# Reordered ScalarE copies and queue writes around the weighted sums, and a shorter last whitening chain

## The chip, the cores and the metric

The kernel runs on one core of one Trainium2 chip. The metric is device time in microseconds (us) of one execution. The profile is that of one further execution, taken by the hardware profiler.

## What is computed

Two layers follow each other. The first is a local attention with learned weights: for every pixel, 49 weights come from two convolutions and a softmax, and they weight the 49 dilated neighbours of that pixel.

```python
# x: (4, 256, 64, 64) f32; w1: (128, 256, 7, 7); w2: (49, 128, 1, 1)
k = conv(x, w1, rhs_dilation=(2, 2), padding 6) + b1
k = conv(k, w2) + b2
attn = softmax(k, axis=1)
xp = pad(x, 6)
shifts = stack([xp[:, :, 2*u:2*u+64, 2*v:2*v+64] for u in range(7) for v in range(7)], axis=1)
x = einsum('bkchw,bkhw->bchw', shifts, attn)
```

The second layer whitens the 256 channels in 4 groups of 64, over all 16384 pixels of the 4 images (m = 16384):

```python
x = x.transpose(1, 0, 2, 3).reshape(4, 64, -1)
xc = x - mean(x)
Sigma = 1e-5 * I + xc @ xc.T / m
rTr = 1 / trace(Sigma);  SN = Sigma * rTr;  P = I
for _ in range(5):
    P = 1.5 * P - 0.5 * (P @ P @ P) @ SN
out = (P * sqrt(rTr)) @ xc * weight + bias
```

## The kernel before

Dilation 2 splits an image into even and odd rows and columns, so the kernel works on 16 parts (`n`, four for each image `b`), each a quarter of an image. The two convolutions are merged into one 7x7 convolution with 49 outputs, and that one is run in a transformed domain: six transformed rows for each image (`ROWS`), each in three banks of transformed columns (`BANKS`, `i` = 0, 1, 2), plus one row that is computed directly (`direct_inf`).

- **Convolution step** (`conv_step`, L828). `conv_bank` (L577) issues the matmuls of a bank (L603) into one of two PSUM buffers `cv`, and ScalarE copies the result to `pv` (L614, L619). `prepare` (L819) makes weights and inputs for the same bank of the next row on VectorE: `row_eval` (L488; for row 0 it has two copies on ScalarE, L510, one for each of the two row parities), `col_eval` (which leaves a copy of one input to ScalarE, L545 or L551), `weights` (L403; for image 1 they are also scaled on ScalarE, L481, and stored for reuse by a DMA on SP, L482). The copies and scalings are put into a list `points` and issued after the eviction of the next bank (L625). VectorE then interpolates (`col_interp`, `row_interp`, L345 to L352).
- **Softmax** (`softmax`, L1037). TensorE transposes the logits (L1009), ScalarE takes exponentials (L1049), VectorE normalises and shuffles (L997).
- **Weighted sums**, part by part. `move_terms` (L1095) lays the weights out in `zt` with eleven copies (L1127, on ScalarE for images 0 to 2), and eight DMAs write them to memory (`sd`, L1146, on GpSimd's queue POOL; for part 12 half of them on SP). `load_band` (L1182) reads them back as bands through SP (L1196, L1208). `first_half` and `second_half` (L1453, L1492) transpose blocks of x (L1252), which ScalarE copies to `xb` and to the edge tiles `xbz` (L1283, L1274); multiply them with the bands (L1316); and store the sums in place of x (L1338).
- **Moments**. `turn_y` (L1382) transposes the stored sums (L1388), ScalarE copies them to `yt` (L1398), and `moments` adds their products to `sig` in PSUM (L1407). In each image one part is closed at once by `finish` (L1444); the others are closed inside the next `first_half`. When the two parts of a tile of x are closed, `move` (L1426) writes the tile to memory (`spill`, 2 MB, POOL) and reads a later image into its place (`slot<-ahead`, 2 MB, L159, POOL).
- **Order of the work.** The parts' steps are planned into gaps between the convolution steps (`plan`, `gap`, L1516 to L1589), eight gaps to an image. Each engine's order is fixed when the program is built: a scheduler takes what is ready, first what stands in `tc.high_priority()`; TensorE keeps program order.
- **End.** After the last convolution the remaining parts run without convolution steps between them (L1616 to L1664). Then two whitening chains (`whiten`, L1706), one for each half of the channels, go through short steps on TensorE, ScalarE and VectorE. The first is filled with the remaining sums (`units`); the second runs between the matmuls of the output (L1701), whose results ScalarE and VectorE scale (L1830, L1836), and SP writes out (L1842, 33 DMAs from six buffers).

Of the kernel before, what the change touches and what calls it, by code (L numbers as in the profile page):

```python
# [32 lines left out]
def kernel(  # L33
# [31 lines left out]
    P = 128  # L65
# [508 lines left out]

    later, points = [], []

    def conv_bank(b, br, i, w):  # L577
# [34 lines left out]
        with tc.high_priority():  # L612
# [5 lines left out]
            if INF in pts:  # L618
# [5 lines left out]
                )  # L624
        for waiting in (points, later) if i == 1 else (points,):  # L625
            while waiting:
                with tc.high_priority() if waiting is points else nullcontext():
                    copied = waiting.pop()()
                for one in copied if isinstance(copied, list) else [copied]:
                    tc.add_manual_dep(  # L630
                        one.ins,
                        last.ins.name,
                        mybir.DependencyInfo(
                            mybir.DependencyClass.NoSync, mybir.DependencyReason.DATA
                        ),
                        reason="later",
                    )

# [189 lines left out]
    def conv_step(k, i):  # L828
        w = {bc: nxt.pop(bc) for bc in BANKS[i]}
        b, br = rows[k]  # L830
        conv_bank(b, br, i, w)
        end = b > 0 and br == ROWS[-1]
        if end:

            with in_order():
                if i == len(BANKS) - 2:
                    col_interp(b, br, 0)
                elif i == len(BANKS) - 1:
                    col_interp(b, br, 1)
                    row_interp(b, 1)  # L840
        last = i == len(BANKS) - 1 and br == ROWS[-2]
        if k + 1 < len(rows):
            with tc.high_priority() if last else nullcontext():
                prepare(k + 1, i, points.append)
# [250 lines left out]
    def move_terms(n, after=None):  # L1095
# [46 lines left out]
        for g in range(CR):  # L1142
            for h in range(2):
                p0 = g * SW + h * TC
                queue = nc.sync if h and n == 4 * (B - 1) else nc.gpsimd
                dma = queue.dma_start(  # L1146
                    bass.AP(
                        tensor=D.tensor,
                        offset=D.offset + h * HS + g * RS,
                        ap=[[LS, TC], [CR * RS, NCH], [1, KS * WS]],  # L1150
                    ),
                    zt[p0 : p0 + TC, R : R + NCH * KS].rearrange(
                        "p (m e) w -> p m (e w)", e=KS
                    ),
                )
                if queue is nc.gpsimd:
                    written[:] = [dma]
# [285 lines left out]

    def finish():  # L1444

        n = open_n.pop()
        for t8 in (2, 3):
            turn_y(n, t8)
        moments(n, 1)
        if n % 2:  # L1450
            move(n // 2)

    def first_half(n):  # L1453
        last = open_n.pop() if open_n else None

        def turn(t8):
            if last is not None:
                turn_y(last, t8)
# [12 lines left out]
        turn(3)  # L1471
        weighted_sum(n, 0, 3)
        weighted_sum(n, 0, 4)
        move_terms(n + 1, store_y(n, 0))
        half_done.add(n)
        load_band(n + 1, 0)
        make_blocks(n, 3, y_dve.get((n, 0))) if (n, (3, 0)) not in blocks else None
        if last is not None:
            moments(last, 1)
            if last % 2:  # L1480
                move(last // 2)

    def bands(n, after=None):
# [7 lines left out]

    def second_half(n, mid=None):  # L1492
        turned = turn_y(n, 0)
        if n % 4 == 3:
            bands(n + 1, turned)
        weighted_sum(n, 1, 0)
        weighted_sum(n, 1, 1)
        turn_y(n, 1)
        weighted_sum(n, 1, 2)
        weighted_sum(n, 1, 3)  # L1500
        weighted_sum(n, 1, 4)
        if mid is not None:
            mid()
        last = store_y(n, 1)
        if n + 1 < 4 * B:
            make_blocks(n + 1, 0, y_dve.get((n, 1)))
        moments(n, 0)
        open_n.append(n)
        done.add(n)
        bands(n + 1, last)  # L1510
# [25 lines left out]
    for b in range(B):  # L1536
# [5 lines left out]
        if b + 2 < B:  # L1542
            for j in range(8):
                plan(b + 1, 2 + j, hs[j])
                if j == 3:

                    plan(b + 1, 2 + j, finish)
        else:
            for j in range(8):
                if b == B - 1 or 3 + j >= NPC:  # L1550
                    rest.append(hs[j])
                else:
                    plan(b + 1, 3 + j, hs[j])
    for b in range(B - 1):
        for j in range(2) if b else ():
            plan(b + 1, b * j, lambda b=b, j=j: soft(b, j))

    slots[4] = store[4]
    pieces = read_x(halves(store[4]), 4, nc.sync)
# [7 lines left out]
    for b in range(1, B):  # L1567
# [13 lines left out]
        j, at, whole = 0, 0, sum(c for c, _ in steps)  # L1581
        for cost, f in steps:
            f()
            while rest_of:
                rest_of.pop()()
            at += cost
            if at * NPC >= (j + 1) * whole:
                gap(b, j)
                j += 1  # L1589
    apool.release()  # L1590
    rpool = ctx.enter_context(tc.tile_pool(name="rp", bufs=1, reuse_waits="tile"))
# [32 lines left out]
    rest[2]()  # L1624
    finish()
    soft_start(1, False)
    move_terms(n + 2)
    for t8 in range(4):
        if (n, (t8, 0)) not in blocks:
            make_blocks(n, t8)  # L1630
    rest[3]()
    rest[4]()
# [21 lines left out]
    with tc.issue_after(stored.ins):  # L1654
# [17 lines left out]
        lambda: turn_part(0, 1, 0),  # L1672
        lambda: turn_part(0, 1, 1),
        lambda: turn_part(1, 1, 0, 0),
        lambda: turn_part(1, 1, 1, 0),
        lambda: moments_part(0, 1, (0, 1)),
# [16 lines left out]
    nc.vector.tensor_tensor(own, ident[:, :GW], ident[:, GW:], ALU.add)  # L1693
    nc.vector.tensor_scalar(eps, own, EPS, None, ALU.mult)
    nc.vector.tensor_scalar(i15, own, 1.5, None, ALU.mult)
    wm, wmx, sc, beta = {}, {}, {}, {}

    def parts_mm(t, lhs, rhs, crossed=False):
        for i, o in ((G0, G1 if crossed else G0), (G1, G0 if crossed else G1)):
# [4 lines left out]
            )  # L1704

    def whiten(cc):  # L1706

# [4 lines left out]
        G = sig[:, cc]  # L1712
        nmu = work.tile([P, 1], F32, tag="nmu", name=f"nmu{cc}")
        nc.scalar.mul(nmu, G[:, GW : GW + 1], -1.0 / NPIX)
        D = small(f"D{cc}")
        nc.scalar.activation(D, own, AF.Copy, scale=nmu)
        dt_ = small(f"dt{cc}")
        nc.vector.tensor_tensor(dt_, G[:, :GW], own, ALU.mult)
        dg = work.tile([P, 1], F32, tag="dg", name=f"dg{cc}")
        nc.vector.tensor_reduce(dg, dt_, AX.X, ALU.add)  # L1720
        mu = work.tile([P, 1], F32, tag="mu", name=f"mu{cc}")
        nc.vector.tensor_scalar(mu, G[:, GW : GW + 1], 1.0 / NPIX, None, ALU.mult)
        nc.vector.tensor_scalar(dg, dg, 1.0 / NPIX, EPS, ALU.mult, ALU.add)
        traced = nc.vector.scalar_tensor_tensor(dg, mu, nmu, dg, ALU.mult, ALU.add)
        fill()
# [8 lines left out]
        with tc.issue_after(traced.ins):  # L1734
            nc.vector.scalar_tensor_tensor(S, G[:, :GW], 1.0 / NPIX, eps, ALU.mult, ALU.add)
        nc.vector.scalar_tensor_tensor(S, t[:, :GW], mu, S, ALU.mult, ALU.add)
        rtr = work.tile([P, 1], F32, tag="rtr", name=f"rtr{cc}")
# [9 lines left out]
        for it in range(1, T_ITERS):  # L1747
# [10 lines left out]
            fill()  # L1758
            yield

# [5 lines left out]
        q = work.tile([P, 1], F32, tag="q", name=f"q{cc}")  # L1766
        nc.scalar.activation(q, rtr, AF.Sqrt)
# [4 lines left out]
        ab = work.tile([P, 2], F32, tag="ab", name=f"ab{cc}")  # L1772
        scale = ab[:, 0:1]
# [30 lines left out]
    for cc in range(NCC):  # L1804
        for b in (3, 2, 1, 0):
# [3 lines left out]
            for k, (r0, nr) in enumerate(rows):  # L1809
# [4 lines left out]
                for pr in range(2):  # L1814
# [62 lines left out]
```

## Time and profile before

| What | Value |
|---|---|
| Median of 3 runs | 682.57 us (680.88 to 682.58) |
| Profiled execution, its own time | 680.68 us |
| its span | 678.7 us |
| TensorE clock granted, mean | 0.996 |
| VectorE busy | 566.3 us (83%) |
| ScalarE busy | 332.7 us (49%) |
| Output DMAs, first issue to the end of the span | 632.5 us to 678.7 us |
| Spill of a 2 MB tile, issue to landing | 9.8 us (the one at 253.3 us) |
| Reload of a 2 MB tile, issue to landing | 9.7 us (the one at 263.6 us) |

The profiled execution took 2.0 us more than its span; that is what lies before and after the traced work. In a timeline, each line is a run of like instructions with its start, its length and, in brackets, how long the engine was idle before it and what ended that. In a table of windows, each line is a stretch with the busy time and instruction count of every engine, the clock, and how busy the 16 DMA engines were. Ends of matmuls are modelled, so a short wait can be hidden inside a busy stretch.

### The profile page before, as it was taken

The page shows a single profiled execution, that of the slowest core. Times are in us where ns is not written, and L with a number is a line of the kernel's source. Part 1 is how long each engine was busy: PE and PEld are TensorE (multiplying, and loading weights), DVE is VectorE, ACT ScalarE, POOL GpSimd, SP SyncE. Part 2 cuts the span into 40 slices and gives each one's busy share as a digit, 9 for nine tenths or more (in the row PEclk, how much of TensorE's full clock was granted, in tenths as well). Part 3 has the DMA queues.
Part 4 walks back from the last instruction along what each step waited for, and adds up shares of the span by engine and source line. Part 5 has one row for each costly group of instructions (what it writes and reads, how often), then busy time and mean ns, then how long its engine had stood idle before and what let it go on. Part 6 is the DMA issues. An engine that isn't in the chain of part 4 may idle for free.

```text
span 678.7 us, 19071 instructions
## 1 busy us (share of the span) xinstructions
PE 648.2 (96%) x7800; PEld 527.6 (78%) x7800; DVE 566.3 (83%) x1240; ACT 332.7 (49%) x862; POOL 117.2 (17%) x177
## 2 busy tenths in 40 slices
PE   6999999999999999999899999999999999999993
PEld 1439573357899988889899998999899999998430
DVE  3699999999389889999999589989998987633673
ACT  1424331023565555566755554464854566634663
POOL 0000550662213020001122020002130203400000
PEclk9999999999999999999999999999999999999998
DMA  8961899993599979313587485027374325649698
GB/s 318 248 162 67 138 262 361 217 185 50 116 208 224 228 160 370 120 60 84 166 269 245 139 279 189 2 67 190 94 199 111 71 63 123 166 98 384 237 404 354
DMA packets 110607, 126.09 MB, mean 186 GB/s; under 512 B 69255, under 2 KB 91896, under 8 KB 109368
## 3 DMA queue, kind: packets, MB, share of 16 engines
q1 hardware_dynamic: 93528, 69.03, 35.3%
q0 software_dynamic: 10944, 37.57, 22.1%
q10 hardware_dynamic: 6048, 18.27, 8.8%
q8 instruction: 61, 1.00, 0.6%
q14 instruction: 26, 0.21, 0.1%
HBM read 78.78 MB, written 52.36 MB: 193 GB/s over the span
## 4 chain that ended last, share of the span: by engine, by line
PE 67%; DVE 19%; ACT 6%; DMA 4%; issue 2%; POOL 0%; ACTq 0%; DVEq 0%; SPq 0%; POOLq 0%
PE cv L603 24%; PE y L1316 10%; PE cv L770 8%; PE acc L770 8%; PE sig L1407 4%; PE tp L1388 3%; DMA out_dram<-out 3%; PE tp L1252 2%; DVE pv L352 2%; DVE zz L352 2%; PE cv L251 2%; DVE xh L352 2%; DVE ct L352 2%; DVE zz L348 1%; DVE zz L345 1%
## 5 line engine op out<-in xcount | busy, mean ns | idle before, releaser
L603 PE MATMUL cv<-xh,wr 128*49 128x128 f32 x4160 | 232.6, 273 | 0.2
L603 PEld LDWEIGHTS cv<-xh,wr 128*49 128x49 f32 x4160 | 226.1, 124 | 3.3 <-issue 1.0
L1146 POOL DMA_DIRECT2D sd<-zt x124 | 65.2, 532 | 334.6 <-ACT zt L1127 269.6
L1316 PE MATMUL y<-band,xb 128*128 128x209 f32 x448 | 93.9, 342 | 4.7 <-ACT xb L1283 2.7
L1316 PEld LDWEIGHTS y<-band,xb 128*128 128x128 f32 x448 | 75.7, 190 | 6.0 <-ACT xb L1283 3.3
L614 ACT COPY pv<-cv 113x486 f32<-113x486 f32 (+2 forms) x60 | 26.0, 433 | 90.6 <-PE cv L603 90.3
L352 DVE SCALAR_TENSOR_TENSOR pv<-pv 113x162 f32<-113x162 f32 x176 | 53.1, 322 | 2.2 <-ACT pv L614 1.4
L1127 ACT COPY zt<-d 32x112 f32<-32x112 f32 (+2 forms) x132 | 38.5, 292 | 14.9 <-DVE d L997 9.3
L1398 ACT COPY yt<-tp 128x512 f32<-128x512 f32 x60 | 34.9, 593 | 21.1 <-PE tp L1388 20.5
L1388 PE MATMUL tp<-ident,slot 128*128 128x128 f32 x240 | 41.5, 296 | 1.0 <-ACT slot L1338 1.0
L1049 ACT ACTIVATE d<-tp,mx 128x49 f32<-128x49 f32 x96 | 27.5, 322 | 28.0 <-DVE mx L1046 28.0
L1252 PE MATMUL tp<-ident,slot 128*128 128x128 f32 x256 | 40.5, 282 | 0.0
L1407 PE MATMUL sig<-yt 128*64 128x65 f32 x1024 | 38.1, 225 | 2.3 <-ACT yt L1398 2.3
L1388 PEld LDWEIGHTS tp<-ident,slot 128*128 128x128 f32 x240 | 34.9, 205 | 6.1 <-issue 3.8
L1407 PEld LDWEIGHTS sig<-yt 128*64 128x64 f32 x1024 | 32.9, 137 | 8.2 <-ACT yt L1398 3.0
L1252 PEld LDWEIGHTS tp<-ident,slot 128*128 128x128 f32 x256 | 38.1, 204 | 0.2 <-issue 0.2
L1283 ACT COPY xb<-tp 128x512 f32<-128x512 f32 x52 | 30.5, 586 | 9.7 <-PE tp L1252 6.6
L352 DVE SCALAR_TENSOR_TENSOR xh<-ct 128x512 f32<-128x512 f32 x40 | 26.5, 692 | 10.2 <-PE cv L603 9.9
L770 PE MATMUL acc<-slot,tap 128*49 128x256 f32 (+7 forms) x224 | 34.7, 468 | 0.0
L770 PEld LDWEIGHTS acc<-slot,tap 128*49 128x49 f32 x224 | 16.0, 123 | 18.0 <-issue 15.5
L147 POOL DMA_DIRECT2D slot<-in_x_dram x12 | 20.4, 1700 | 53.8 <-DVE xh L352 38.2
L348 DVE TENSOR_TENSOR pv<-pv 113x162 f32<-113x162 f32 (+1 forms) x77 | 27.5, 366 | 0.3
(258 smaller groups left out, 1141.2 us busy)
## 6 DMA issues: line engine op xcount, KB each, us to landing
out_dram<-out SPq DMA_DIRECT2D x31, 512.0 KB, 5.9
band<-sd SPq DMA_DIRECT2D x64, 242.0 KB, 3.7
sd<-zt POOLq DMA_DIRECT2D x124, 77.0 KB, 3.3
wr<-gd ACTq DMA_DIRECT2D x14, 588.0 KB, 5.0
wr<-gd ACTq DMA_DIRECT2D x14, 490.0 KB, 4.8
slot<-in_x_dram POOLq DMA_DIRECT2D x12, 512.0 KB, 10.5
ahead<-in_x_dram POOLq DMA_DIRECT2D x12, 512.0 KB, 7.5
spill<-slot POOLq DMA_DIRECT2D x3, 2048.0 KB, 10.5
```

Source lines behind the costliest of these rows:

```text
L348: return in_turn(TT(o, a, b, ALU.subtract))
L352: return in_turn(STT(o, a, f, b, ALU.mult, ALU.add))
L603: nc.tensor.matmul(o, wv[:, sc, sr, cc], xv[bc][:, h * NCC + cc], start=(j == 0), stop=(j == len(terms) - 1), skip_group_check=True,)
L770: nc.tensor.matmul(ps[h * HB : h * HB + KT, :, o0:o1], w[v][:, cc], rhs, start=(j == 0 and k == 0), stop=(j == len(order) - 1), skip_group ...
L1127: ins = nc.scalar.copy(o, i)
L1146: dma = queue.dma_start(bass.AP(tensor=D.tensor, offset=D.offset + h * HS + g * RS, ap=[[LS, TC], [CR * RS, NCH], [1, KS * WS]],), zt[p0 : ...
L1252: nc.tensor.transpose(t[:, h * C + cc * P : h * C + (cc + 1) * P], tile_of(xt, cc, t8, h, pc), turned_by(n),)
L1283: (nc.vector.tensor_copy if n > 4 * B - 3 else nc.scalar.copy)(xb.rearrange("p a c -> p (a c)"), t[:, : 2 * C])
L1316: nc.tensor.matmul(y_ps[n, half, cc][:, q0 : q0 + nq, c0:c1], xb[:, cc * P : (cc + 1) * P], rhs, start=(k == 0), stop=(k == len(PIECES[hal ...
L1388: nc.tensor.transpose(t[:, h * C + cc * P : h * C + (cc + 1) * P], tile_of(yt, cc, t8, h, pc), turned_by(n),)
L1398: return nc.scalar.copy(yb.rearrange("p h a g c -> p (h a g) c")[:, :, :GW], t[:, : 2 * C].rearrange("p (e c) -> p e c", c=GW),)
L1407: nc.tensor.matmul(sig[g * GW : (g + 1) * GW, cc], yb[:, g, :GW], yb[:, g], start=(count[0] == 0), stop=end, skip_group_check=True,)
```

## The change

It touches the order around the weighted sums, the POOL and SP queues, and the end. No matmul, tile size or buffer count is changed.

1. **Held copies.** When the gap after a step holds one half of a part's sums (`half_gaps`), the copies and scalings in `points` are no longer issued behind the eviction ahead of that gap. They go to `held`, and `give_out` issues them after a `turn_y` or a store inside the half. For the first bank of row 0 of an image, `prepare` itself is called after such a gap (`after_gap`).
2. **Closing a part.** `finish` is called inside `second_half` (`close=True`), ahead of the `move_terms` of the next part, no longer as a step of its own after it. So ScalarE copies `yt` before `zt`, and the spill and the reload move up in POOL's queue: the spill now stands ahead of the eight `sd` writes of parts 3 and 7, and the reload behind the first of them and ahead of the other seven.
3. **Part 4** writes half of its eight `sd` pieces through SP, as part 12 did.
4. **First block.** The block transpose and `xb` copy of part 0 are planned one gap earlier.
5. **After the convolutions.** One part's last moments are put after the sums of the following first half (`ends`), so the logits' transposes come earlier.
6. **Whitening.** The negated mean is dropped; the mean is scaled so that the division by the pixel count falls out, which drops an operation on ScalarE and one on VectorE ahead of the trace. Two one-column operations are added (on `qi`, and `down`), and the last two operations for `beta` become one. Two `turn_part` copies go from ScalarE to VectorE.
7. **Fillers.** The last two fillers stand behind output tiles 2 and 3 instead of 1 and 2, and the second chain skips one output tile and drops its last stop.

In the built program the instruction counts of TensorE stay at 4215. On ScalarE 808 instructions become 804, on VectorE 1202 become 1204.

```diff
-        for waiting in (points, later) if i == 1 else (points,):
...
+        if half_next[0]:
+            held.extend(points)
+            points.clear()
+        give_out(points, last)
+        if i == 1:
+            give_out(later, last)
...
+            if half_next[0] and (i, rows[k + 1][1]) == (0, 0):
+                after_gap.append(lambda: prepare(k + 1, i, points.append))
+            else:
+                with tc.high_priority() if last else nullcontext():
+                    prepare(k + 1, i, points.append)
...
-                queue = nc.sync if h and n == 4 * (B - 1) else nc.gpsimd
+                queue = nc.sync if h and n in (4, 4 * (B - 1)) else nc.gpsimd
...
+        if turned is not None:
+            give_out(held, turned)
+        stored = store_y(n, 0)
+        give_out(held, stored)
+        move_terms(n + 1, stored)
...
-    def second_half(n, mid=None):
+    def second_half(n, mid=None, close=False):
...
+        give_out(held, turned)
...
         moments(n, 0)
         open_n.append(n)
+        if close:
+            last = finish()
         done.add(n)
         bands(n + 1, last)
...
-                plan(b + 1, 2 + j, hs[j])
-                if j == 3:
-
-                    plan(b + 1, 2 + j, finish)
+                half_gaps.add((b + 1 + (2 + j) // NPC, (2 + j) % NPC))
+                plan(b + 1, 2 + j, (lambda f=hs[j]: f(None, True)) if j == 3 else hs[j])
...
+    plan(1, 1, lambda: make_blocks(0, 0))
...
-    finish()
+    ends = []
+    finish(ends)
     soft_start(1, False)
...
-    rest[3]()
+    rest[3](ends.pop())
...
-        lambda: turn_part(0, 1, 1),
+        lambda: turn_part(0, 1, 1, on=nc.vector.tensor_copy),
...
-        nc.scalar.mul(nmu, G[:, GW : GW + 1], -1.0 / NPIX)
+        nc.vector.tensor_scalar(mu, G[:, GW : GW + 1], 1.0 / ROOT, None, ALU.mult)
         D = small(f"D{cc}")
-        nc.scalar.activation(D, own, AF.Copy, scale=nmu)
+        nc.scalar.activation(D, own, AF.Copy, scale=mu)
...
-        nc.vector.tensor_scalar(dg, dg, 1.0 / NPIX, EPS, ALU.mult, ALU.add)
-        traced = nc.vector.scalar_tensor_tensor(dg, mu, nmu, dg, ALU.mult, ALU.add)
+        traced = nc.vector.scalar_tensor_tensor(dg, mu, mu, dg, ALU.mult, ALU.subtract)
...
-            yield
+            if it < T_ITERS - 1:
+                yield
...
+        nc.vector.tensor_scalar(qi, qi, -float(NPIX), None, ALU.mult)
...
+        nc.vector.tensor_scalar(down, scale, -1.0 / ROOT, None, ALU.mult)
...
-        nc.vector.tensor_scalar(bt, t[:, :1], scale, -1.0, ALU.mult, ALU.mult)
-        nc.vector.tensor_tensor(bt, bt, shift_sb[:, cc : cc + 1], ALU.add)
+        nc.vector.scalar_tensor_tensor(
+            bt, t[:, :1], down, shift_sb[:, cc : cc + 1], ALU.mult, ALU.add
+        )
...
-                if idx in (1, 2):
+                if idx in (2, 3):
                     units.pop(0)()
-                if idx > LEAD + 1:
+                if idx > LEAD + 1 and idx != LEAD + 3:
                     next(chains[1], None)
```

More of the change, by code (lines that the diff above doesn't have):

```diff
@@ L573 @@
     slot = {}
-    later, points = [], []
+    later, points, held = [], [], []
+    half_next, half_gaps, after_gap = [False], set(), []
     def conv_bank(b, br, i, w):
@@ L624, in conv_bank, with give_out @@
                 )
-        for waiting in (points, later) if i == 1 else (points,):
[L626 to L637, printed above, removed]
+        if half_next[0]:
[4 more added lines that the diff above has]
+            give_out(later, last)
+    def give_out(waiting, last):
+        while waiting:
+            with nullcontext() if waiting is later else tc.high_priority():
+                copied = waiting.pop()()
+            for one in copied if isinstance(copied, list) else [copied]:
+                tc.add_manual_dep(
+                    one.ins,
+                    last.ins.name,
+                    mybir.DependencyInfo(
+                        mybir.DependencyClass.NoSync, mybir.DependencyReason.DATA
+                    ),
+                    reason="later",
+                )
     def interpolate(pt, tmp, outs, cut, part=None, pairs=None):
@@ L842, in conv_step @@
         if k + 1 < len(rows):
-            with tc.high_priority() if last else nullcontext():
-                prepare(k + 1, i, points.append)
+            if half_next[0] and (i, rows[k + 1][1]) == (0, 0):
[3 more added lines that the diff above has]
+                    prepare(k + 1, i, points.append)
         if i == len(BANKS) - 1 and not end:
@@ L1442, with finish, end, first_half @@
     half_done = {-1}
-    def finish():
+    def finish(late=None):
         n = open_n.pop()
         for t8 in (2, 3):
[L1448 to L1453, printed above, removed]
+            turned = turn_y(n, t8)
+        def end():
+            moments(n, 1)
+            if n % 2:
+                move(n // 2)
+        end() if late is None else late.append(end)
+        return turned
+    def first_half(n, end=None):
         last = open_n.pop() if open_n else None
         def turn(t8):
-            if last is not None:
-                turn_y(last, t8)
+            return turn_y(last, t8) if last is not None else None
         def block(t8):
@@ L1470, in first_half @@
         weighted_sum(n, 0, 2)
-        turn(3)
+        turned = turn(3)
         weighted_sum(n, 0, 3)
         weighted_sum(n, 0, 4)
-        move_terms(n + 1, store_y(n, 0))
+        if turned is not None:
[3 more added lines that the diff above has]
+        move_terms(n + 1, stored)
         half_done.add(n)
@@ L1481, in first_half @@
                 move(last // 2)
+        if end is not None:
+            end()
     def bands(n, after=None):
@@ L1497, in second_half @@
         weighted_sum(n, 1, 1)
-        turn_y(n, 1)
+        turned = turn_y(n, 1)
         weighted_sum(n, 1, 2)
@@ L1552 @@
                 else:
+                    half_gaps.add((b + 1, 3 + j))
                     plan(b + 1, 3 + j, hs[j])
@@ L1582 @@
         for cost, f in steps:
+            half_next[0] = (at + cost) * NPC >= (j + 1) * whole and (b, j) in half_gaps
             f()
@@ L1589 @@
                 j += 1
+                while after_gap:
+                    after_gap.pop()()
     apool.release()
@@ L1672 @@
         lambda: turn_part(0, 1, 0),
-        lambda: turn_part(0, 1, 1),
+        lambda: turn_part(0, 1, 1, on=nc.vector.tensor_copy),
         lambda: turn_part(1, 1, 0, 0),
-        lambda: turn_part(1, 1, 1, 0),
+        lambda: turn_part(1, 1, 1, 0, nc.vector.tensor_copy),
         lambda: moments_part(0, 1, (0, 1)),
@@ L1693 @@
     nc.vector.tensor_tensor(own, ident[:, :GW], ident[:, GW:], ALU.add)
-    nc.vector.tensor_scalar(eps, own, EPS, None, ALU.mult)
+    nc.vector.tensor_scalar(eps, own, NPIX * EPS, None, ALU.mult)
     nc.vector.tensor_scalar(i15, own, 1.5, None, ALU.mult)
@@ L1704, in parts_mm @@
             )
+    ROOT = NPIX**0.5
     def whiten(cc):
@@ L1712, in whiten @@
         G = sig[:, cc]
-        nmu = work.tile([P, 1], F32, tag="nmu", name=f"nmu{cc}")
-        nc.scalar.mul(nmu, G[:, GW : GW + 1], -1.0 / NPIX)
+        mu = work.tile([P, 1], F32, tag="mu", name=f"mu{cc}")
+        nc.vector.tensor_scalar(mu, G[:, GW : GW + 1], 1.0 / ROOT, None, ALU.mult)
         D = small(f"D{cc}")
-        nc.scalar.activation(D, own, AF.Copy, scale=nmu)
+        nc.scalar.activation(D, own, AF.Copy, scale=mu)
         dt_ = small(f"dt{cc}")
-        nc.vector.tensor_tensor(dt_, G[:, :GW], own, ALU.mult)
+        nc.vector.scalar_tensor_tensor(dt_, G[:, :GW], NPIX * EPS, own, ALU.add, ALU.mult)
         dg = work.tile([P, 1], F32, tag="dg", name=f"dg{cc}")
         nc.vector.tensor_reduce(dg, dt_, AX.X, ALU.add)
-        mu = work.tile([P, 1], F32, tag="mu", name=f"mu{cc}")
-        nc.vector.tensor_scalar(mu, G[:, GW : GW + 1], 1.0 / NPIX, None, ALU.mult)
-        nc.vector.tensor_scalar(dg, dg, 1.0 / NPIX, EPS, ALU.mult, ALU.add)
-        traced = nc.vector.scalar_tensor_tensor(dg, mu, nmu, dg, ALU.mult, ALU.add)
+        traced = nc.vector.scalar_tensor_tensor(dg, mu, mu, dg, ALU.mult, ALU.subtract)
         fill()
@@ L1734, in whiten @@
         with tc.issue_after(traced.ins):
-            nc.vector.scalar_tensor_tensor(S, G[:, :GW], 1.0 / NPIX, eps, ALU.mult, ALU.add)
-        nc.vector.scalar_tensor_tensor(S, t[:, :GW], mu, S, ALU.mult, ALU.add)
+            nc.vector.tensor_tensor(S, G[:, :GW], eps, ALU.add)
+        nc.vector.scalar_tensor_tensor(S, t[:, :GW], mu, S, ALU.mult, ALU.subtract)
         rtr = work.tile([P, 1], F32, tag="rtr", name=f"rtr{cc}")
@@ L1766, in whiten @@
         q = work.tile([P, 1], F32, tag="q", name=f"q{cc}")
-        nc.scalar.activation(q, rtr, AF.Sqrt)
+        nc.scalar.activation(q, rtr, AF.Sqrt, scale=-float(NPIX))
         qi = work.tile([P, 1], F32, tag="qi", name=f"qi{cc}")
@@ L1770, in whiten @@
             nc.vector.reciprocal(qi, q)
+        nc.vector.tensor_scalar(qi, qi, -float(NPIX), None, ALU.mult)
         nc.vector.scalar_tensor_tensor(q, qi, rtr, q, ALU.mult, ALU.add)
-        ab = work.tile([P, 2], F32, tag="ab", name=f"ab{cc}")
-        scale = ab[:, 0:1]
+        ab = work.tile([P, 3], F32, tag="ab", name=f"ab{cc}")
+        scale, down = ab[:, 0:1], ab[:, 2:3]
         nc.vector.scalar_tensor_tensor(
@@ L1780, in whiten @@
         bt = ab[:, 1:2]
[L1781 to L1782 removed]
+        nc.vector.scalar_tensor_tensor(
+            bt, t[:, :1], down, shift_sb[:, cc : cc + 1], ALU.mult, ALU.add
+        )
         sc[cc], beta[cc] = scale, bt
```

## The prediction, made before the run

> **What bounds the kernel now.** I read the page's totals first, then its chain, then what the waits of TensorE (PE) end on, then PE's timeline.
>
> ```profile
> PE 648.2 (96%) x7800; PEld 527.6 (78%) x7800; DVE 566.3 (83%) x1240; ACT 332.7 (49%) x862; POOL 117.2 (17%) x177
> ```
>
> ```profile
> PE 67%; DVE 19%; ACT 6%; DMA 4%; issue 2%; POOL 0%; ACTq 0%; DVEq 0%; SPq 0%; POOLq 0%
> ```
>
> PE is busy 96% of 678.7 us and makes two thirds of the chain. No matmul goes, so what can be won is PE's idle time, and after 632 us the wait for the output. The waits of PE (sum, count, mean) name ScalarE (ACT) copies at 49% load: an order problem, not a load problem.
>
> ```profile
> PE y L1316 <- ACT xb L1283: 2.7, 3, 1.1
> PE sig L1407 <- ACT yt L1398: 2.3, 4, 0.8
> PE y L1316 <- DMA band<-sd: 1.9, 2, 1.3
> PE y L1316 <- ACT xbz L1274: 1.4, 2, 1.1
> ```
>
> PE's timeline places them (start, length; in brackets the idle time before it and what ended it):
>
> ```profile
> 190.97 0.97 PE L1316 MATMUL y<-band,xb 128*128 128x209 f32 x4 [1.09 <-ACT xb L1283]
> ...
> 246.77 1.18 PE L1407 MATMUL sig<-yt 128*64 128x65 f32 x32 [0.82 <-ACT yt L1398]
> ...
> 331.75 0.98 PE L1316 MATMUL y<-band,xb 128*128 128x209 f32 x4 [1.30 <-DMA band<-sd]
> ...
> 481.37 0.98 PE L1316 MATMUL y<-band,xb 128*128 128x209 f32 x4 [0.85 <-ACT xb L1283]
> ```
>
> From 190 to 640 all such brackets sum to 9.9 us, plus 1.08 at 640.35 (the second whitening chain). The last stage has another limit, shown by two of its windows (length; busy time of PE, PEld, DVE, ACT, POOL; clock, DMA share, GB/s):
>
> ```profile
> 634.00:636.00 2.00, 2.00 (x24) 0.82 (x24) 1.45 (x2) 1.32 (x2) 0.00 (x0) 1.00 0.63 243
> 646.00:668.00 22.00, 20.11 (x182) 7.23 (x176) 15.32 (x27) 14.35 (x22) 0.00 (x0) 1.00 1.02 406
> ```
>
> From 646 us the DMA engines are full at 406 GB/s. There only an earlier first output, or fewer gaps between outputs (634 to 636 and 642 to 644), moves the end.
>
> **What the Trainium skill says.** "PSUM — Partial Sum Buffer", Engine vs sequencer instructions: an engine's queue is strictly first in, first out. The trace agrees: the `xb` copy that PE waits for at 481 starts behind a copy for the convolution.
>
> ```profile
> 479.39 0.74 ACT L545 COPY xh<-rb 128x512 f32<-128x512 f32 x1
> ...
> 480.64 0.68 ACT L1283 COPY xb<-tp 128x512 f32<-128x512 f32 x1
> ```
>
> "DMA: Bandwidth & Descriptors", Issuing engines are not separate DMA queues: issuing from more engines saves only sequencer time. Eight `sd` issues took POOL 4.29 us, four took SP 1.88. Same page, Queues, rings and completion order: a DMA engine takes a ring's descriptors in order. So a 2 MB transfer moved ahead of `sd` writes holds them back; no row of before has them in that order. Same page, Bandwidth: the ceiling is about 435 GB/s; 406 in the tail is near it.
>
> **The change part by part.** In the built program I compared each engine's order with that of before.
>
> *First block (point 4) and held copies at 190.* The convolution ends at 189.14, the next begins at 195.84: 6.70 us. Between them stand four block transposes, waited on through an `xb` copy, and the sums. With the transposes a gap earlier and the L545 copy held, I rebuild the stretch from its own rows to 4.66 us; the transposes (0.47) are paid earlier, where ACT is idle for their copy. 6.70 − 4.66 − 0.47 = 1.57: −1.5 (−1.0 to −1.6).
>
> *Closing (point 2).* At 246.77 and 387.58 the moments waited 0.82 and 0.79 for `yt`, behind five `zt` copies:
>
> ```profile
> 244.61 1.50 ACT L1127 COPY zt<-d 128x56 f32<-128x56 f32 x5
> 246.13 1.07 ACT L1398 COPY yt<-tp 128x512 f32<-128x512 f32 x2
> ```
>
> `yt` now goes first. I take 0.65 of each: −1.3 (−0.8 to −1.6). `zt` is some 1.07 later; its band is needed over 10 us later, which hides it. The `spill` moves up to about 244 and 385, and the reload behind it stands ahead of seven `sd` writes: a rival below.
>
> *Held copies at 481.* Waits of 0.85 and 0.35 behind L545 (0.74): −1.1 (−0.5 to −1.2). I price the held copies themselves at nothing: their inputs `xh` are read 2 to 10 us after the new place (one made by 326.6 is read at 338.7). Without that cover each would cost its 0.6 to 0.75 us at the next convolution. The first bank of rows 0, whose `prepare` follows the gap, has some 5 us of VectorE (DVE) work shifted; the logits it delays stand several us before their first reader.
>
> *Part 4 (point 3).* Band waits of 0.65 and 1.30 at 329 and 331.75. The eight issues end at 324.07 on POOL; split four and four, at about 322 (part 12: 1.88 on SP, 2.12 on POOL). The band read at 325.48 then starts 1.1 to 2.1 us earlier: −1.5 of 1.95 (−0.6 to −1.95). SP has nothing urgent queued there.
>
> *Held copies at 264.68 and 293.38* (1.09, 0.78). Nothing (−0.5 to +0.5). In the built order an L510 copy (1.05 us) still stands between the `xbz` copies of the first, and the `xb` of the second stays behind the L481 scaling, which waits for DVE's `wr`; DVE is full from 252.4 to 291.
>
> *After the convolutions (point 5).* Waits of 0.25, 0.58 and 0.22 from 570.92 to 579.14. Moments behind the sums fill the wait for the stored `slot`; the logits come 1.35 us earlier: −0.8 (−0.3 to −1.05).
>
> *Whitening and fillers (points 6, 7).* The front of the first chain is paced by its fillers on PE, so most dropped operations save nothing; one DVE operation (0.25, start to start) goes ahead of the first output. The two added one-column operations (0.36 together) and the two `turn_part` copies (0.43 each) lie in DVE idle time of about 0.6. With the fillers one tile later, outputs 1 and 2 come some 0.45 earlier, which shortens the DMA gap at 634 to 636 by about 0.3; the gap at 642 to 644 (0.42) goes, as PE has an output tile to do where it waited 1.08. 0.25 + 0.3 + 0.42: −1.0 (−0.2 to −1.5).
>
> Sum: −1.5 − 1.3 − 1.1 − 1.5 − 0 − 0.8 − 1.0 = −7.2. The gains before 632 lie on PE's own path, so they add and shift the tail; what they expose next is the DVE stage after 252, which starts when PE frees its weights and so moves with PE. The profiled execution took 680.68 (span 678.7 + 2.0): 680.68 − 7.2 = 673.5. The median of the runs is 1.9 above it: 682.57 − 7.2 = 675.4. The parts' half-widths (0.3, 0.4, 0.35, 0.7, 0.5, 0.4, 0.65), as independent errors, give ±1.3; with the spread of the median, 0.7 on the fast side and 0.8 on the slow, 673.4 to 677.5.
>
> **Rivals.**
> *The gains are absorbed in part.* The stage from 252 to 291 is DVE's; if it starts no earlier, the 1.5 at 190 and 0.65 at 247 are lost in it, and half of part 4's to the `xb` copy. 7.2 − 1.5 − 0.65 − 0.75 = 4.3: 678.3. For it: DVE is 83% busy. Against: at 252.42 DVE starts after 3.29 us idle, ended by PE's `cv`.
>
> *The change doesn't do what it says.* The next ACT copy or band takes the place of each wait removed, as I expect at 264 and 293, and only the tail's 1.0 stays: 681.5. Against: at 190, 247 and 387 the copy ahead is one that leaves, and ACT is half idle.
>
> *Slower: the reload of part 3's tile comes late.* Spill and reload took 9.8 and 9.7 us from 253.3 on. Started at 244.3 with the same durations, the reload lands at 263.8. But from 244 to 253 the DMA engines are already 92% busy, with small packets (159 GB/s):
>
> ```profile
> 244.00:253.00 9.00, 8.18 (x164) 7.92 (x162) 5.61 (x16) 5.53 (x18) 3.89 (x8) 1.00 0.92 159
> ```
>
> The ACT copy that reads the new slot (L510, 278.25 before) now stands at about 267.6 in ACT's queue, ahead of the `pv` evictions; I work out 4.6 us of ACT work behind it, needed by about 276.9, so a landing after some 271.5 stops ACT and then PE, one for one. With the engines shared evenly I estimate a landing near 270.5, just inside. At half rate throughout, the two take 39 us in place of 19.5 and land at 283.3, 11.8 us late: 682.57 − 7.2 + 11.8 = 687.2. It decides the sign from a landing at about 279. For it: these shares. Against: shares of 0.92 (244 to 253), 0.96 (to 264) and 1.00 (to 274) are 28.8 us of engine time for everything, the two transfers included, so later than 274 means engine time lost, not shared. A landing at 274 costs 2.5 us and is part of the absorbed case. The seven `sd` writes behind the reload, in ring order, would then land some 5 us later (my estimate from eight writes of 77 KB at the 135 GB/s of 248 to 250), and the band read after them is needed at 290. Part 7's pair, moved to 385, meets shares of 0.54.
>
> **How the numbers follow.** Forecast 675.4: 0.64. Absorbed 678.3: 0.20. No effect 681.5: 0.09. Slower 687.2: 0.07, of which 0.01 is a delay that only takes up part of the gain. Beyond 0.3% (2.0 us, about what a measurement of this kernel can tell from no change): faster 0.64 + 0.20 + 0.01 = 0.85; same 0.09; slower 0.06. The range reaches to the absorbed case with 0.9 added for run spread, 679.2, and on the low side to 672.8, where the uncosted waits hidden in PE's busy stretches would show. It leaves out no effect, slower (0.16 together) and little else.
>
> **What would show it.** PE's brackets at about 190, 246, 386, 330, 479 and 570 to 577 gone or under 0.3; those at 264 and 293 still there. POOL's `spill` right after the store of parts 3 and 7. First output some 6.5 us earlier than 632.5, then DMA share near 1 without a gap at 642 to 644. The slower rival: ACT idle in front of L510, ended by the DMA `slot<-ahead`. I am wrong in the mechanism if PE's idle sum from 190 to 640 stays above 6 us, or if DVE idles less and PE more after 252.

## The result, and the profile after

| | Kernel before | Changed kernel |
|---|---|---|
| Median | 681.84 us (680.88 to 682.58, 4 runs) | 672.39 us (672.28 to 672.52, 4 runs) |
| Profiled execution, its own time | 680.68 us | 672.28 us |
| its span | 678.7 us | 670.5 us |

The ratio is 0.9862, with a 95% interval of 0.9845 to 0.9879: 9.45 us less, where 7.2 was forecast, and 0.4 us below the low end of the range. In all the runs made beside the experiments the kernel before spread from 680.45 to 684.64 (64 runs, median 681.3); from that median the gain is 8.9 us. From profile to profile the span fell by 8.2.

The page's totals and chain of the changed kernel, and then its waits of TensorE:

```profile
PE 647.9 (97%) x7800; PEld 528.4 (79%) x7800; DVE 567.2 (85%) x1242; ACT 331.3 (49%) x858; POOL 115.0 (17%) x173
```

```profile
PE 81%; DVE 10%; DMA 4%; ACT 2%; issue 1%; POOL 0%; SPq 0%; DVEq 0%; ACTq 0%; POOLq 0%
```

```profile
PE y L1328 <- ACT xbz L1286: 1.1, 1, 1.1
...
PE sig L1419 <- ACT yt L1410: 0.9, 3, 0.4
...
PE y L1328 <- ACT xb L1295: 0.6, 1, 0.6
```

TensorE is busy as long as before, its share of the chain rose from 67% to 81%, and the waits for the band are gone from the list (L1328 is the old L1316, L1295 the old L1283, and so on: lines after the first edits stand some 10 lower). In the timeline of TensorE only these brackets are left from 190 us to the end of the convolutions:

```profile
244.95 1.18 PE L1419 MATMUL sig<-yt 128*64 128x65 f32 x32 [0.25 <-ACT yt L1410]
262.87 0.69 PE L1328 MATMUL y<-bandz,xbz 128*128 128x96 f32 x4 [1.10 <-ACT xbz L1286]
291.36 0.98 PE L1328 MATMUL y<-band,xb 128*128 128x209 f32 x4 [0.55 <-ACT xb L1295]
382.61 1.17 PE L1419 MATMUL sig<-yt 128*64 128x65 f32 x32 [0.25 <-ACT yt L1410]
```

The matmuls of the convolution, the same in both kernels, serve as marks: how much earlier each comes tells where the time went. Each row is a stretch from the last convolution matmul ahead of the sums to the first one behind them, except where it names other marks.

| Stretch (time before) | Before | Changed | Difference | Forecast |
|---|---|---|---|---|
| 189: first block, held copy (0.49 of it paid at 179) | 6.77 | 5.03 | −1.25 net | −1.5 |
| 239 and 380: closing | 9.21, 9.18 | 8.64, 8.63 | −1.12 | −1.3 |
| 289: sums in the VectorE stage | 8.68 | 8.47 | −0.2 | 0 |
| 328: part 4 | 9.46 | 7.00 | −2.46 | −1.5 |
| 453: inside a convolution | 11.84 | 11.52 | −0.32 | none |
| 477: held copy | 8.71 | 7.08 | −1.63 | −1.1 |
| 541 to the first output matmul: moments moved | | | −1.67 | −0.8 |
| first output matmul to the end of the span | 47.6 | 47.9 | +0.3 | −1.0 |

The first output matmul comes at 622.63 in place of 631.12, 8.49 earlier; the differences above it sum to −8.65, and small drifts in the convolutions give 0.2 back. The idle times in brackets from 190 us to the first output sum to 9.90 us before and to 3.25 after, 6.65 less: the gain is larger than the idle time that went. Of the 8.49, 8.2 reaches the end of the span: in this trace the output takes 0.3 longer. That can't be told from chance: in the nine traces with the old end, before and eight of the runs below, the same stretch takes 47.2 to 48.2.

### The profile page after: what moved, and what is told of

Read it like the earlier page. It is cut to its first block, busy times and chain, and to the rows that moved or that the text cites. A ratio compares the mean times of both kernels' runs of the same rounds, so it can differ in the third digit from the quotient of the medians.

```text
span 670.5 us, 19066 instructions
## 1 busy us (share of the span) xinstructions
PE 647.9 (97%) x7800; PEld 528.4 (79%) x7800; DVE 567.2 (85%) x1242; ACT 331.3 (49%) x858; POOL 115.0 (17%) x173
## 4 chain that ended last, share of the span: by engine, by line
PE 81%; DVE 10%; DMA 4%; ACT 2%; issue 1%; POOL 0%; SPq 0%; DVEq 0%; ACTq 0%; POOLq 0%
PE cv L604 30%; PE y L1328 13%; PE cv L779 10%; PE acc L779 8%; PE sig L1419 5%; PE tp L1400 4%; PE tp L1264 4%; DMA out_dram<-out 3%; PE cv L251 2%; DVE zz L352 1%; DVE pv L352 1%; PE tp L1021 1%; DVE zz L348 1%; PE tp L1730 1%; DVE ct L352 1%
## 5 line engine op out<-in xcount | busy, mean ns | idle before, releaser
L1158 POOL DMA_DIRECT2D sd<-zt x120 | 63.0, 532 | 294.9 <-ACT zt L1139 232.0
L1328 PE MATMUL y<-band,xb 128*128 128x209 f32 x448 | 93.8, 342 | 0.6 <-ACT xb L1295 0.6
L1328 PEld LDWEIGHTS y<-band,xb 128*128 128x128 f32 x448 | 75.9, 191 | 1.3 <-ACT xb L1295 0.7
L1295 ACT COPY xb<-tp 128x512 f32<-128x512 f32 x52 | 30.6, 589 | 8.9 <-PE tp L1264 5.7
```

The source lines that it names most:

```text
L1158: dma = queue.dma_start(bass.AP(tensor=D.tensor, offset=D.offset + h * HS + g * RS, ap=[[LS, TC], [CR * RS, NCH], [1, KS * WS]],), zt[p0 : ...
L1295: (nc.vector.tensor_copy if n > 4 * B - 3 else nc.scalar.copy)(xb.rearrange("p a c -> p (a c)"), t[:, : 2 * C])
L1328: nc.tensor.matmul(y_ps[n, half, cc][:, q0 : q0 + nq, c0:c1], xb[:, cc * P : (cc + 1) * P], rhs, start=(k == 0), stop=(k == len(PIECES[hal ...
```

## The experiments

Times are medians. The kernel before had 681.25 beside the first four, 681.76 beside the next four, 681.46 beside the last four; so differences under about 0.5 between sets are not read.

### Each point alone

**Point 3 alone: the split over two queues.**

```diff
-                queue = nc.sync if h and n == 4 * (B - 1) else nc.gpsimd
+                queue = nc.sync if h and n in (4, 4 * (B - 1)) else nc.gpsimd
```

> The kernel before, with part 4's second half of the sd writes on SP and nothing else changed. Theory 1 (a stop of TensorE costs the idle time that the timeline puts in brackets plus some 0.26 us: about 0.16 in the group before it and 0.10 in the group after it, as start-to-start times of the two traces give): the stretch from the last convolution matmul before part 4's sums to the first one after them goes from 9.46 to 7.00 us, so 2.45 us less than a run of before at its lower level. Theory 2 (the stops are worth what the brackets say, and the rest of the surplus came from the other parts): 1.5 to 1.95 less. Theory 3, on the spread of the runs of before (two levels, 680.9 to 681.1 and 682.6): it comes from these two band waits, so the runs of this kernel lie within 0.3 us; if it comes from elsewhere, they still show two levels 1.5 us apart.

Measured: 681.29 (680.15 to 682.34), ratio 0.9994 (0.9983 to 1.0004). Nothing in the medians. In its profile part 4's stretch is 8.38, 1.1 shorter than before and 1.4 longer than in the changed kernel; but that execution, with 680.28, is among the shortest of the 14, and of the 0.9 that its first output comes earlier, 0.7 is gone at the end (47.55 before from there to the end, 48.24 here). Its TensorE timeline at that place:

```profile
330.23 0.98 PE L1328 MATMUL y<-band,xb 128*128 128x209 f32 x4 [0.53 <-DMA band<-sd]
333.91 0.69 PE L1328 MATMUL y<-bandz,xbz 128*128 128x96 f32 x4 [0.34 <-ACT xbz L1286]
```

One band wait remains, and a ScalarE copy is the next wait behind it. The trace shows where the forecast goes wrong: the eight issues end at 322.3, as forecast, but the first read starts at 325.26, only 0.2 earlier than before, and the second at 325.86, 0.9 earlier. The writes landed 2.6 to 4.0 us after their issue, where before it took 2.5 to 3.2. Both theories of the size fall: something else shortened part 4's stretch in the changed kernel. The spread narrowed to 2.2 us but did not go; no run reaches 682.4, where 12 of the 44 beside it lie.

**Point 1 alone: held copies.** Of all points, only `half_gaps` with `held` and `after_gap` are kept.

> The kernel before, with the held copies alone. Theory 1 (bracket plus 0.26 for each stop): two stops at 481 to 484, 0.85 and 0.35 in brackets, give 1.63 to 1.72; at 190 the xb copy starts about 0.7 earlier; some 0.3 in a stop near 464: together 2.6 us less than before. Theory 2 (brackets alone): 1.1 to 1.2 at 481 and 0.7 at 190, about 1.9. Rival 3: the copies held back stop the convolution after the gap, and the gain is under 1.

Measured: 679.33 (678.61 to 680.98), ratio 0.9971 (0.9962 to 0.998): 1.9 less. The stretch at 477 went from 8.71 to 7.51 and the one at 189 from 6.77 to 6.36, 1.6 together. A bracket of 0.28 stays at 480, so the first theory's 2.6 was too much; the 1.9 is the second theory's number, but by another sum: one stop of 0.85 shrank to 0.28, and one of 0.35 went. The copies held back stopped nothing: every convolution takes as long as before.

**Point 2 alone: closing.**

```diff
-                plan(b + 1, 2 + j, hs[j])
-                if j == 3:
-                    plan(b + 1, 2 + j, finish)
+                plan(b + 1, 2 + j, (lambda f=hs[j]: f(None, True)) if j == 3 else hs[j])
```

> The kernel before, with the close of parts 3 and 7 ahead of the next weights' copies, and with what that moves in POOL's queue. Theory 1: two stops shrink from 0.82 and 0.79 to about 0.25 each, 1.1 us less than before; the spill and the reload cost nothing. Theory 2 (the prediction's size): 1.3 less. Rival 3: the reload, started about 8 us earlier among the small packets, stops ScalarE in front of the L510 copy; the time is then no lower than before.

Measured: 676.5 (676.16 to 676.84), ratio 0.9924 (0.991 to 0.9937): 4.75 less, some four times what the theories gave it. The two `yt` stops shrank as expected (−0.58 and −0.55). But part 4's stretch, some 80 us after the one and 60 before the other, fell from 9.46 to 7.79, with all eight `sd` writes still on POOL. The 0.2 at 289 and the 0.32 at 453 are there too, and 0.36 at 477, which the table lays to the held copy alone. And its six runs lie within 0.7 us.

**Point 5 alone: the last moments later.**

```diff
-    finish()
+    ends = []
+    finish(ends)
...
-    rest[3]()
+    rest[3](ends.pop())
```

> The kernel before, with the one part's last moments behind the following half's sums after the convolutions. Theory 1 (bracket plus 0.26 a stop, three stops of 0.25, 0.58 and 0.22): 1.6 to 1.8 us less. Theory 2 (the prediction's size): 0.8 less, at most 1.05. Rival 3: the output at the end is bound by its own chain and gives nothing back: 0.

Measured: 679.75 (678.69 to 682.74), ratio 0.9976 (0.9966 to 0.9987): 1.5 less; the stretch from 541 on fell by 1.64. Theory 1 holds.

The profile of this run fell on a long execution (682.41). Up to part 4 its order is that of before, and it shows one thing that makes the runs spread. Windows of it, and then its TensorE timeline:

```profile
330.00:332.00 2.00, 0.98 (x7) 0.79 (x6) 2.00 (x6) 0.97 (x3) 0.00 (x0) 1.00 0.86 261
332.00:334.00 2.00, 0.76 (x4) 0.76 (x5) 2.00 (x6) 0.37 (x1) 0.00 (x0) 1.00 0.38 97
334.00:336.00 2.00, 2.00 (x11) 1.85 (x10) 2.00 (x5) 1.24 (x3) 0.00 (x0) 0.66 0.80 247
336.00:338.00 2.00, 2.00 (x9) 1.97 (x8) 2.00 (x7) 0.67 (x2) 0.00 (x0) 0.50 0.00 1
338.00:340.00 2.00, 2.00 (x41) 1.86 (x42) 2.00 (x4) 1.55 (x3) 0.00 (x0) 0.99 0.01 4
```

```profile
329.54 0.97 PE L1328 MATMUL y<-band,xb 128*128 128x209 f32 x4 [1.04 <-DMA band<-sd]
...
333.24 0.97 PE L1328 MATMUL y<-band,xb 128*128 128x209 f32 x4 [2.27 <-DMA band<-sd]
334.06 0.63 PE L1264 MATMUL tp<-ident,slot 128*128 128x128 f32 x4
334.53 1.49 PE L1328 MATMUL y<-band,xb 128*128 128x209 f32 x4
```

The band behind the longer wait took 6.4 us to land here, 5.0 in the profile of before, and the two waits are 3.31 in place of 1.95. Then the clock column (the third number from the right) falls to 0.66 and 0.50, and a group of four matmuls takes 1.49 where it took 0.88. From 333.24 to the next convolution are 6.80 us, against 5.15 in before: the lower clock cost 1.65. The two windows say the same: 2.00 × 0.34 + 2.00 × 0.50 = 1.68 us of clock are missing. The stretch is 12.46, 3.0 longer.

### What closing did to part 4

At that place closing changed the order of ScalarE, and of a few VectorE instructions. ScalarE in the kernel before:

```profile
315.26 0.86 ACT L1127 COPY zt<-d 128x56 f32<-128x56 f32 x3 [3.55 <-DVE d L997]
316.14 1.39 ACT L1338 ACTIVATE slot<-y,pivot_x 128x512 f32<-128x512 f32 x2
317.38 0.58 ACT L1283 COPY xb<-tp 128x512 f32<-128x512 f32 x1
317.98 2.48 ACT L1127 COPY zt<-d 32x112 f32<-32x112 f32 x8
```

ScalarE stands 3.55 us at part 4's first `zt` copies, which wait for VectorE's shuffle of `d`, and the two stores and an `xb` copy, which could run, stand behind them and then between the `zt` copies. I tried the other order alone: the kernel before, in which part 3 now asks for part 4's bands only after its stores.

```diff
-        if n % 4 == 3:
+        if n % 4 == 3 and n != 3:
             bands(n + 1, turned)
```

In the built program this moves two stores and one `xb` copy ahead of three `zt` copies, and nothing else on any engine.

> The kernel before with one difference in the built order: on ScalarE, ahead of part 4, the two stores and one xb copy of part 3 stand in front of three zt copies in place of behind them. Theory A (this order is what closing made cheap at part 4, and what makes the runs of before spread: ScalarE stood at zt, which waited for VectorE's shuffle, with the store behind it): what closing alone gained beyond its two yt waits and smaller stops, 4.75 - 2.0 = 2.7 us, comes back here: about 678.5, and the runs lie within 0.8 us. Rival B (closing gained it by the queue order on POOL or on VectorE): no gain here, 681.2, and the spread stays.

Measured: 678.61 (678.14 to 679.02), ratio 0.9952 (0.9938 to 0.9966). Theory A holds in both. The median is 3.15 below its own runs of before, of which 5 in 11 lie above 682.4, and 2.7 below the median of all 64; the spread is 0.9 us. ScalarE of this run:

```profile
312.89 1.35 ACT L1338 ACTIVATE slot<-y,pivot_x 128x512 f32<-128x512 f32 x2 [1.14 <-PE y L1316]
314.12 0.57 ACT L1283 COPY xb<-tp 128x512 f32<-128x512 f32 x1
315.31 3.35 ACT L1127 COPY zt<-d 128x56 f32<-128x56 f32 x11 [0.61 <-issue]
```

The `zt` copies start when they did, but end at 318.66 in place of 320.46: 1.8 us earlier, because the stores were done in the time that ScalarE had spent waiting. The `sd` writes start at 317.99 (319.78 before), the second band read starts at 325.36 (326.71 before) and lands in 3.1 us, and part 4's stretch is 6.97, without a bracket. One queue is enough.

**Closing and the split together** (points 2 and 3).

> The kernel before with closing (points 2) and the split of part 4 over SP and POOL (point 3) together. Theory A (the split saves issue time on the path only once the zt copies come early): the rest of the wait of 0.54 at part 4 goes with its 0.26, 0.8 us less than closing alone: 675.7. Rival B (the split gives nothing, as alone): 676.5.

Measured: 676.75 (676.66 to 677.04). Rival B: the split adds nothing. The band wait of 0.54 went and a wait of 0.34 for an `xbz` copy came, with the same stretch of 7.80.

**The changed kernel without the split** (point 3 undone).

> The changed kernel with all eight sd writes of part 4 on POOL again (point 3 undone). Theory A (once the zt copies stand behind the stores, the band comes in time even from one queue, as the kernel before with the stores first showed): within 0.3 us of the changed kernel, 672.1 to 672.7, and runs as close together. Theory B (the prediction's size): 1.5 more, 673.9.

Measured: 672.35 (672.12 to 672.76). Theory A. By the medians, point 3 is worth nothing in any of three surroundings.

### The other parts of the changed kernel

**Without the early first block** (point 4 undone: the planned `make_blocks(0, 0)` is left out).

> The changed kernel without the early first block (point 4 undone). Theory A (bracket plus 0.26 for the stop at 190, less the 0.45 for the block's matmuls that were paid earlier; the held copy alone took 0.41 of it): 1.74 - 0.41 - 0.45 = 0.9 more, 673.3. Rival B (the stage of VectorE from 252 on takes it up): within 0.3, 672.1 to 672.7.

Measured: 673.16 (672.82 to 673.4), 0.8 more. Theory A; the VectorE stage after 252 did not take it up.

**With the old end** (points 6 and 7 undone).

> The changed kernel with the whitening chains and fillers of before (points 6 and 7 undone). Theory A (the end is paced by the output's DMA, and the fillers only move its gaps): within 0.4 us of the changed kernel, 672.0 to 672.8. Theory B (the prediction's): the end was worth 1.0, so 673.4.

Measured: 672.0 (671.71 to 672.15). The end was worth nothing; theory A. Windows of the output in the kernel before, and then those of the changed kernel 8.5 us earlier, show why:

```profile
636.00:638.00 2.00, 2.00 (x19) 0.67 (x12) 1.77 (x8) 1.95 (x6) 0.00 (x0) 1.00 0.98 391
638.00:640.00 2.00, 1.27 (x11) 0.38 (x10) 1.93 (x6) 0.89 (x3) 0.00 (x0) 1.00 0.98 387
...
642.00:644.00 2.00, 1.80 (x24) 0.60 (x18) 1.63 (x4) 1.45 (x3) 0.00 (x0) 1.00 0.79 297
```

```profile
625.50:627.50 2.00, 2.00 (x28) 0.83 (x24) 0.86 (x2) 0.78 (x1) 0.00 (x0) 1.00 0.92 363
627.50:629.50 2.00, 1.76 (x18) 0.34 (x9) 1.76 (x7) 1.88 (x4) 0.00 (x0) 1.00 0.83 336
629.50:631.50 2.00, 2.00 (x20) 1.00 (x20) 1.93 (x7) 1.08 (x3) 0.00 (x0) 1.00 0.86 348
...
633.50:635.50 2.00, 1.42 (x20) 0.86 (x24) 1.51 (x5) 0.47 (x2) 0.00 (x0) 1.00 0.75 299
```

The share of the DMA engines (the number before the last) rose from 0.63 at 634 to 0.92 at 625.5, as forecast, but the next two fell from 0.98 and 0.98 to 0.83 and 0.86, where the fillers now stand, and the gap of 0.79 at 642 is still there at 633.5 with 0.75. TensorE waits for the second chain as long as it did: 1.07 us at 634.08 for `PS`, where it had waited 1.08 at 640.35 for `qi`. Over the 14 us after the first output the missing share is 2.6 us in both.

**With the old fillers only** (half of point 7 undone).

> The changed kernel with its new whitening chains and the fillers behind output tiles 1 and 2 again (half of point 7 undone). Theory A (the fillers only move the DMA's gaps): within 0.4, 672.0 to 672.8; if the fillers' new place is what cost the 0.4 that undoing the whole end gave back, 672.0. Theory B (the prediction's): 0.3 more, 672.7.

Measured: 672.37 (672.2 to 672.5): the place of the fillers is worth nothing either way.

**The two waits that are left.** The first L510 copy goes behind the stores at 262, the L481 scalings behind those at 294, and the order at part 4 is written in as above.

```diff
-                nc.scalar.copy(r[2], xs[:, 0])
+                copied = nc.scalar.copy(r[2], xs[:, 0])
+                if last_store:
+                    tc.add_manual_dep(copied.ins, last_store[0].ins.name, ...)
```

> The changed kernel with its two longest waits taken out in the order of ScalarE: the first L510 copy behind the store in the sums at 257 to 264, the L481 scalings behind the store in the sums at 288 to 296, and the stores ahead of zt at part 4 written in as an order. Theory A (a stop costs bracket plus 0.26, and TensorE stays the bound): 1.10 + 0.26 + 0.55 + 0.26 = 2.2 us less than the changed kernel, 670.2. Rival B (that stage is bound by VectorE, as the prediction said when it put nothing there): no gain, 672.4, or a loss of up to 1 where the L510 copy comes too late for VectorE.

Measured: 671.74 (671.58 to 671.76), ratio to before 0.985 (0.9834 to 0.9867): 0.65 below the changed kernel, between the theories. At 262 the stop of 1.10 went and the stretch fell from 6.33 to 4.97, by 1.36, as theory A has it. But the wait at 291 grew:

```profile
290.61 0.98 PE L1340 MATMUL y<-band,xb 128*128 128x209 f32 x4 [1.05 <-ACT xb L1307]
```

```profile
288.38 0.72 ACT L757 ACTIVATE lgx<-lgx,bias 113x512 f32<-113x512 f32 x1 [2.70 <-DVE lgx L352]
289.01 0.57 ACT L802 COPY zz<-cv 113x512 f32<-113x512 f32 x1
289.48 0.59 ACT L1423 COPY yt<-tp 128x512 f32<-128x512 f32 x1
289.96 0.60 ACT L1307 COPY xb<-tp 128x512 f32<-128x512 f32 x1
```

ScalarE waits for VectorE's `lgx` until 288.38, within 0.1 of the time in the changed kernel (288.31), and `yt` and `xb` stand behind. So rival B holds from there: part of a gain ahead of VectorE's full stage is given back at its end. Another 0.28 goes at part 4, whose stretch is 7.28 here; I did not look into that.

**These orders with the old end.**

> The kernel of the last waits (first L510 copy, L481 scalings and stores at part 4 in the order written in), with the old whitening chains and fillers. Theory A (the two differences add): 671.7 - 0.4 = 671.3, the fastest so far. Rival B (the end is worth nothing either way): 671.7.

Measured: 671.86 (671.61 to 671.97). The two do not add: rival B. The fastest kernel stays the one before it, at 671.74.

## Why the prediction was right and wrong

The sign and the bound were right: TensorE paced the kernel until 632, and gains before it added up and moved the end. The median came 3.0 us below the forecast of 675.4. Of that, 1.8, the largest part, is the offset between median and profile, which the forecast carried over (1.9) and the changed kernel does not have (0.1), and 1.2 is the sum of the parts (8.4 between the two profiled executions, 7.2 forecast). This sum hides larger errors that in part cancel: the end gave nothing of its 1.0, and the terms for 328, 477 and 541 were 2.4 too small together. Point by point:

- **Part 4 (point 3)** is the step that failed: "split four and four, at about 322 ... The band read at 325.48 then starts 1.1 to 2.1 us earlier: −1.5 of 1.95". With the split alone that read started 0.2 us earlier, as the writes took longer to land, and the median did not move. The 2.46 of this stretch came from a ScalarE order that closing changed as a side effect: with that order alone the stretch is as short as in the changed kernel (6.97 and 7.00). I had compared the built orders, and costed closing only where it was aimed. With ScalarE's strict queue, which I had quoted for 481, the line at 315.26 with its 3.55 us could have told it: what stands behind a wait for VectorE is late.
- **The size of a stop.** I took the bracket as the most that a removed wait can give. One stop shows more. In before, the transposes at 329.82 and the sums at 331.75 start 1.93 apart; in the changed kernel the same two groups start 0.47 apart:

```profile
329.82 0.63 PE L1252 MATMUL tp<-ident,slot 128*128 128x128 f32 x4
```

```profile
326.90 0.64 PE L1264 MATMUL tp<-ident,slot 128*128 128x128 f32 x4
327.37 0.87 PE L1328 MATMUL y<-band,xb 128*128 128x209 f32 x4
```

That is 1.46 for a bracket of 1.30. And the group after the stop lasts 0.81 to the next start (332.56), in place of 0.71 (328.08). So this stop cost its bracket and some 0.26: 0.16 before it, which I lay to the end of the last matmuls that is no longer hidden, and 0.10 after it. The Trainium skill, "TensorE: Matmul & The Clock Gate", Single matmul latency, gives about 175 ns for the drain of a single bf16 matmul; the 0.16 is near that, but no run here shows that it is the same thing. Taken as a rule for a stop that goes entirely, the 0.26 was tried elsewhere: the stop of 1.10 at 262 gave 1.36 when it went, as worked out ahead; the three from 571 to 579 are 1.05 + 0.78 = 1.8 (measured 1.67); those at 481 and 484 are 1.7 (1.63). Part 4's 1.95 + 0.52 = 2.47 (2.46) is no test, as the 0.26 was read there. "Half-widths" that ended at the bracket could not hold these.
- **The median.** "The median of the runs is 1.9 above it: 682.57 − 7.2 = 675.4" carried the offset of before over to a kernel that has none: the changed kernel's profile, 672.28, is 0.1 from its median. The offset comes from long executions of before. Of its 64 runs, 20 lie from 682.45 to 684.64 and the others at or below 681.81; every run of the upper group has a mean clock of 0.991 to 0.993, and every other 0.994 to 0.996. The 1.68 us of clock that part 4's stops cost in the long trace above are 0.0025 of 680, about the distance between the groups. Held copies alone and moments moved alone, which leave part 4's waits, have such runs too (8 of 19 and 5 of 18, at 0.993 or less); the split alone (14 runs), closing alone, closing with the split, and the stores first (18 runs together) have none. So part 4's wait is the likely cause; that the clock fell there was seen in one trace. Against the profiled execution the forecast was 673.5 and the result 672.28.
- **The end**, forecast at −1.0, is the other step that failed: it was +0.3 in the profiles, and nothing in the medians. The operation dropped ahead of the first output gave 0.05 in place of 0.25 (541 to the first output: 88.96 with the old end, 88.91 with the new). The first output's gap shrank as I said, and the work moved into the next windows: I had priced the fillers where they left and not where they went. And the wait of 1.08, which an output tile was to fill, moved along the chain and stayed.
- **First block, closing, held copies at 190** were right in place and near in size. (The parts closed at 244 and 385 are 1 and 5; it is the `sd` writes behind them that belong to parts 3 and 7.) At 262 and 293, where nothing was forecast, −0.2 came; that the L510 copy stays in the way and that VectorE sets the end of that stage were both shown by the run on the last waits. The VectorE reorder that I laid to the held copies belongs to closing: alone, the held copies change no order there. Why 0.32 went inside the convolution at 453 I have not settled; closing alone has it.
- **Rivals.** The slower one's mechanism showed itself once and cost nothing:

```profile
400.89 1.05 ACT L510 COPY rb<-slot 128x1024 f32<-128x1024 f32 x1 [1.42 <-DMA slot<-ahead]
```

The reloads took 9.1 to 11.9 us, not twice their time. L510 waited 1.42 for the last of them, and TensorE lost nothing by it: its stretch at 400 takes 5.14 us in both kernels. The room of the forecast was worked out for the first reload, which landed at 261.6, ahead of the copy that reads it (265.48). The `sd` writes behind the reloads were held back as the forecast's ring order has it: the first seven landed 8.2 to 9.3 us after their issue (2.4 to 3.3 before), from 261.98 on, just behind the reload. Their bands still came in time.

## What to carry to other kernels

In an in-order queue, look for an engine standing long at an instruction while ready work is behind it, even if that engine is half idle and the one that pays is 10 us and two DMAs away. Compare the built orders everywhere, not only where the edit is aimed. Where a stop of TensorE goes entirely, try a price above the idle time shown, and don't carry a median's offset over before you know what makes it.

## What the runs showed of the hardware

- After two stops of 1.04 and 2.27 us with 1.4 us of matmuls between them, the granted clock stood at half for some 3.4 us (worked out from the two windows), which cost 1.65 us; after stops of 0.65 and 1.30 (before) and of 1.11 and 0.99 (held copies alone) it did not fall. "TensorE: Matmul & The Clock Gate", What's actually happening, tells of a clock at half rate after an idle window of about 3.4 us; the half rate agrees, but here neither stop alone was that long.
- Reads of part 4's band of the same 242 KB took 2.6 to 6.4 us to land. The time of issue alone does not order them: the second read of the pair took 3.1 us when issued at 325.36 (stores first), 4.3 at 323.26 (changed kernel without the split), 5.0 at 326.71 (before) and 6.4 at 326.79 (moments moved). What stands beside them I did not take apart. In this way a small delay on ScalarE can become a larger one for TensorE: with copies that ended 1.8 us earlier, that read was issued 1.35 earlier and landed 3.2 earlier (328.51, 331.70 before), which was worth 2.5 in the profile's stretch and some 2.7 in the medians.
